# A sparse graph-attention stack on one core: the first layer's weight load placed behind the first edge list

## The chip, the core and the metric

The kernel runs on one core of a Trainium2 chip. The metric is device time in microseconds of one execution, lower is better. Five engines work in parallel, each on its own queue of instructions: TensorE (PE, matmuls), VectorE (DVE), ScalarE (ACT), GpSimd (POOL) and SyncE (SP, which here only issues transfers). DMA engines move data between the device's main memory and the on-chip memories.

## What is computed

The inputs are x (4096 nodes by 512 features), a 4096 by 4096 adjacency of zeros and ones, and weights. Two residual blocks follow each other; cut to what matters:

```python
# layer 0: 8 heads of width 64
h  = einsum('nf,kfp->knp', x, W)
f1 = einsum('knp,kp->kn', h, a[:, :64, 0]); f2 = einsum('knp,kp->kn', h, a[:, 64:, 0])
e  = where(adj > 0, leaky_relu(f2[:, :, None] + f1[:, None, :], 0.2), -1e16)
x  = layernorm(x + heads_side_by_side(softmax(e) @ h))
# layer 1: a graph attention of 8 heads with elu, one of a single head of width 512 with elu,
#          then relu(out @ lin1_w + lin1_b) @ lin2_w + lin2_b
x  = layernorm(x + layer1(x, adj))
```

The adjacency is sparse, with degrees that fall with the index of the node, so tile 0 (the first 128 nodes) has by far the most edges. For each node the sum over its neighbours is all that the softmax needs.

## The kernel before

The kernel works with lists of edges. Nodes come in 32 tiles of 128. It has three stages.

**Stage 1** (`find_edges`, with `beside` for what is done next to it) makes the lists and projects x. The rows of a tile are looked at in *parts*: tile 0 has four (columns 0 to 256, to 1024, to 2304, to 4096), every other tile has one, so there are 35 parts, v = 0 to 34. A part goes through these steps:

- `signs_of` brings the adjacency rows (`raw`) in and ACT turns them into signs (`sg`, L848). For tile 0 this is done in eight pieces ahead of everything else (`sg0`).
- PE makes keys from signs and column numbers (L877, L878) in PSUM.
- DVE searches each segment of columns for its largest keys, eight at a time: MAX8 into `cand` (L884), MATCH_REPLACE8 into `left` (L887), and so on. For tile 0 a segment takes three rounds. `left` has two buffers, and `cand` of tile 0 has one, so that the search of its next part waits for the list of the one before.
- DVE merges the candidates into one sorted list `lst`: MAX8 (L899) and MATCH_REPLACE8 (L901) in turn; part 0 has 13 rounds.
- ACT, POOL and PE turn the list into positions: qs and signs (L906, L909), degs and counts (L911 to L928), a prefix sum prs (L931), sides (L942, L943), s1 (L944), and pl (L960 to L969). ACT copies a column of it, kk (L984). DVE picks the neighbours' numbers (L977 to L988), and POOL writes them to `idx` (L991 to L994).

After the last part of a tile comes `beside(t)`: x's rows of that tile (`xr`) are loaded, transposed on PE (L683), copied by ACT (`xt`, L686), multiplied with the layer's weights on PE (`ph`, L697), copied to a row by ACT (L710) and written to a table in main memory by SP (L711). At t = 8 and t = 16 it loads the weights of the other two attention layers.

`load_projection` brings a layer's weights into `st.w` (eight transfers of 128 KB, L654, for layers of eight heads) and appends columns to them: for each of two attention vectors, broadcast to all partitions (`sab`, L663), and each of four chunks, POOL multiplies weights and vector (`sprod`, L667, 128 by 512 elements) and DVE sums each head's 64 products (L672; L677 for the layer of one head). That makes eight products and eight sums for a layer. `sprod` has two buffers, so a product waits for the sum two before it.

**Order.** In stage 1 the order of each engine's queue is not written by hand. A planner fixes it when the kernel is built: it walks through time by its own estimates of durations, and when an engine is free it takes, of the instructions whose inputs are then ready, the one that stands first in the program. Steps that stand late in the program are taken early where nothing else is ready: the second layer's sums, which stand at tile 8, run from 69 to 78 us here, among the second part of tile 0. On the chip the queue then runs in that order, whatever is late. Memory of closed pools is used again; the buffers of one layer's load lie where those of another did.

**Stages 2 and 3** gather table rows by `idx` with indirect transfers (L1084), weigh them on DVE (L1208) and sum them by matmuls (L1220). Their order is written out in the code, and no line of theirs is touched. The part of stage 1 that the change concerns:

Of the kernel before, what the change touches and what calls it, by code (L numbers as in the profile page):

```python
# [558 lines left out]
def sparse_path(  # L559
# [78 lines left out]
    st0 = Stage2("t0", 8, 64, dest_first=False)  # L638
# [5 lines left out]
    def load_projection(pool, st, w, a):  # L644

        hs, dm = st.heads, st.dim


        st.w = pool.tile([P, FC, 2, st.wide], F32, name=f"sw_{st.name}")
        for c in range(FC):  # L650
            for j in range(2):
                mine = st.w[:, c, j, :HF]
                if hs > 1:
                    nc.sync.dma_start(  # L654
                        mine.rearrange("p (k o) -> p k o", o=dm),
                        w[ts(j, hs // 2), ts(c, P), :].rearrange("k f o -> f k o"),
                    )
                else:
                    nc.sync.dma_start(mine, w[0, ts(c, P), ts(j, HF)])
        with tc.tile_pool(name=f"swload_{st.name}", bufs=2) as wp:  # L660
            for side in range(2):
                ab = wp.tile([P, hs, dm], F32, name="sab")
                nc.sync.dma_start(ab, a[:, ts(side, dm)].partition_broadcast(P))  # L663
                d = (side == 1) == st.dest_first
                for c in range(FC):
                    prod = wp.tile([P, 2, HF], F32, name="sprod")
                    nc.gpsimd.tensor_mul(  # L667
                        prod, st.w[:, c, :, :HF], ab.rearrange("p h d -> p (h d)").rearrange("p (j f) -> p j f", j=2)
                    )
                    if hs > 1:  # L670
                        at = HF if d else HF + hs // 2
                        nc.vector.tensor_reduce(  # L672
                            st.w[:, c, :, at : at + hs // 2],
                            prod.rearrange("p j (h d) -> p j h d", d=dm), AX.X, OP.add,
                        )
                    else:
                        nc.vector.tensor_reduce(st.w[:, c, int(d), HF:], prod, AX.XY, OP.add)  # L677

    def turn_in(sb, ps, st, src, t):

        pt = ps.tile([P, FC, P], F32, name="pt", tag="ph")
        for c in range(FC):
            nc.tensor.transpose(pt[:, c, :], src[:, ts(c, P)], ident)  # L683
        xt = sb.tile([P, FC, P], F32, name="xt")
        for c in range(FC):
            nc.scalar.activation(  # L686
                xt[:, c, :], pt[:, c, :], AF.Copy, accum_out=st.xparts[:, c, t : t + 1]
            )
        return xt

    def project_in(ps, st, columns, n=P):

        halves = []
        for j in range(2):
            ph = ps.tile([P, st.wide], F32, name="ph")
            for c in range(FC):
                nc.tensor.matmul(ph[:n], columns(c), st.w[:, c, j], start=(c == 0), stop=(c == FC - 1))  # L697
            halves.append(ph)
        return halves
# [35 lines left out]
    def project_mean(sb, ps, st):  # L735

        mean = sb.tile([P, FC], F32, name="mean")
        nc.vector.tensor_reduce(mean, st.xparts, AX.X, OP.add)
        nc.vector.tensor_scalar_mul(mean, mean, 1.0 / N)
        project_out(sb, st, project_in(ps, st, lambda c: mean[:, c : c + 1], 1), NT, 1)  # L740
# [99 lines left out]
    def signs_of(sb, t, pieces=1):  # L840

        raw = sb.tile([P, N], I32, name="raw", bufs=2)
        sg = sb.tile([P, N], BF16, name="sg")
        w = N // pieces
        for i in range(pieces):
            nc.sync.dma_start(raw[:, ts(i, w)], adj[ts(t, P), ts(i, w)])
        for i in range(pieces):
            nc.scalar.activation(sg[:, ts(i, w)], raw[:, ts(i, w)], AF.Sign)  # L848
        return sg

    def find_edges(big, sb, ps, pk, constants, sg, beside):
# [12 lines left out]
        for v, p in enumerate(pts):  # L864
            t, k, c0, nch = p.t, p.k, p.first, p.n
# [91 lines left out]
            for lo in range(0, nch, per):  # L957
                m = min(per, nch - lo)
                pl = ps.tile([P, m, k + 2], F32, name="pl")
                nc.tensor.matmul(  # L960
                    pl, ident_b, own_b[:, None, kmax - k :].to_broadcast([P, m, k + 2]), start=True, stop=False
                )
                last = None
                for block, groups, chunks in blocks_in(p, lo, m):
                    for of, w in ((rhs, k + 2), (rest, k + 1)):
                        if last:
                            nc.tensor.matmul(*last, start=False, stop=False)
                        last = pl[:, chunks, :w], s1[:, ts(p.at + block, P)], of[:, groups, :w]
                nc.tensor.matmul(*last, start=False, stop=True)  # L969
                cs = slice(c0 + lo, c0 + lo + m)  # L970
                nc.scalar.copy(nl[:, cs], pl[:, :, k + 1])
                nc.gpsimd.tensor_scalar(hole[:, cs, 0], nl[:, cs], -0.5, FAR, op0=OP.is_lt, op1=OP.mult)
                src = sb.tile([P, longest], F32, name="src")[:, :m]
                sel = sb.tile([P, 512], F32, name="sel")[:, : m * k].rearrange("p (m k) -> p m k", k=k)
                if k < 100:
                    shape = [P, m, k]
                    nc.vector.tensor_tensor(  # L977
                        sel, iota_k[:, lo : lo + m, :k], pl[:, :, k : k + 1].to_broadcast(shape), op=OP.is_equal
                    )
                    nc.vector.tensor_tensor(sel, sel, pl[:, :, :k], op=OP.mult)  # L980
                    nc.vector.tensor_reduce(src, sel, AX.X, OP.add)
                else:
                    kk = sb.tile([P, longest], F32, name="kk")[:, :m]
                    nc.scalar.copy(kk, pl[:, :, k])  # L984
                    for c in range(m):
                        nc.vector.scalar_tensor_tensor(
                            sel[:, c], iota_k[:, lo + c, :k], kk[:, c : c + 1], pl[:, c, :k],
                            op0=OP.is_equal, op1=OP.mult, accum_out=src[:, c : c + 1],  # L988
                        )

                past = sb.tile([P, longest], F32, name="past")[:, :m]  # L991
                nc.gpsimd.tensor_scalar(past, nl[:, cs], -0.5, 2.0 * N, op0=OP.is_lt, op1=OP.mult)
                nc.gpsimd.tensor_add(past, past, src)
                nc.gpsimd.tensor_copy(idx[:, cs], past)  # L994
            if p.last:
                beside(t)

# [21 lines left out]
    def blocks_in(p, lo, m):  # L1019


        out = []
        for i in range(p.blocks):
            mine = [(g, c - lo) for g, c in enumerate((i, p.off + i)) if i < p.chunks[g] and lo <= c < lo + m]
            if len(mine) == 2:
                out.append((i, slice(0, 2), slice(mine[0][1], mine[1][1] + 1, p.off)))
            elif mine:
                g, c = mine[0]
                out.append((i, slice(g, g + 1), slice(c, c + 1)))
        return out  # L1030
# [339 lines left out]
    with ExitStack() as pools:  # L1370
        big = pools.enter_context(tc.tile_pool(name="eb", bufs=1))
        sb = pools.enter_context(tc.tile_pool(name="es", bufs=2))
        sg0 = signs_of(sb, 0, 8)
        constants = edge_constants(big)
        load_projection(big, st0, w0, a0)
        ps = pools.enter_context(tc.tile_pool(name="ep", bufs=1, space=PSUM))
        pp = pools.enter_context(tc.tile_pool(name="eq", bufs=2, space=PSUM))
        pk = pools.enter_context(tc.tile_pool(name="ek", bufs=2, space=PSUM))

        def beside(t):  # L1380
            xr = sb.tile([P, F], F32, name="xr")
            nc.sync.dma_start(xr, x[ts(t, P), :])
            xt = turn_in(sb, pp, st0, xr, t)
            project_out(sb, st0, project_in(pp, st0, lambda c: xt[:, c, :]), t)
            if t % 8 == 7:
                split_s(sb, st0, t - 7, 8)
            if t == 8:
                load_projection(late, st1, w1, a1)
            if t == 16:
                load_projection(late, st2, wo, ao)  # L1390

        find_edges(big, sb, ps, pk, constants, sg0, beside)
        project_mean(sb, pp, st0)
# [224 lines left out]
```

## Time and profile before

| | us |
|---|---|
| median of three runs | 2126.52 (2125.99 to 2130.2) |
| the profiled execution, its own time | 2338.45 |
| its span, first to last instruction | 2336.3 |
| busy: PE / DVE / ACT / POOL | 1771.7 / 1331.3 / 660.7 / 1151.6 |
| mean granted TensorE clock | 0.879 |

The profiled execution is 212 us longer than the median, so its microseconds serve to compare places within it. In a timeline each line gives the start, the duration, the engine, the line of the kernel, the operation, what is written from what, and shapes; in brackets stands how long the engine sat idle before it and what released it. A list of waits gives, for each pair of waiting and releasing lines, the total in microseconds, how often, and the longest.

### The profile page before, as it was taken

What the parts mean: (1) busy time and instruction counts of PE and PEld (TensorE: products, weight loads), DVE (VectorE), ACT (ScalarE), POOL (GpSimd) and SP (SyncE); (2) the same over time, 40 slices, a digit from 0 to 9 for tenths busy, and PEclk for the clock granted to TensorE, in tenths of its full rate; (3) what the DMA queues carried; (4) which work ended last, traced back from release to release, by engine and by line L of the source; (5) the groups of instructions that cost most, each with busy time, mean ns of one, the idle gap of its engine ahead of it and who ended that gap; (6) DMA issues with size and microseconds to landing.
All of it is one profiled execution on the core that took longest, in us unless ns stands there. A gap on an engine that the chain in (4) does not pass through costs nothing.

```text
span 2336.3 us, 29301 instructions
## 1 busy us (share of the span) xinstructions
PE 1771.7 (76%) x8987; PEld 1040.1 (45%) x8987; DVE 1331.3 (57%) x3933; ACT 660.7 (28%) x2316; POOL 1151.6 (49%) x1658
## 2 busy tenths in 40 slices
PE   4777776645677787764667687666999898998997
PEld 3655442213444564432444465434545443444444
DVE  5887777745676797744555676653343424334322
ACT  3446776650222222111222232211111011111221
POOL 5424444456555666536556666536355634445300
PEclk9889997866878899876788899887999998999999
DMA  6434565536666667526555556436254624335301
GB/s 214 132 129 158 219 241 220 213 83 179 181 175 182 197 208 224 166 76 163 154 140 145 159 158 186 133 110 191 85 156 126 172 82 148 101 109 150 90 19 51
DMA packets 132589, 351.94 MB, mean 151 GB/s; under 512 B 41922, under 2 KB 42954, under 8 KB 128454
## 3 DMA queue, kind: packets, MB, share of 16 engines
q0 software_dynamic: 74160, 206.25, 32.5%
q1 hardware_dynamic: 58262, 143.72, 17.3%
q8 instruction: 74, 1.21, 0.2%
q14 instruction: 93, 0.76, 0.1%
HBM read 347.31 MB, written 42.24 MB: 167 GB/s over the span
## 4 chain that ended last, share of the span: by engine, by line
PE 46%; DVE 16%; issue 13%; ACT 7%; another core or an unknown queue 7%; POOL 6%; DMA 4%; SPq 0%; DVEq 0%; POOLq 0%; ACTq 0%
PE acc L1220 15%; PE ph L697 11%; PE p L1495 10%; PE p L1507 5%; DVE g L1208 3%; POOL g L1084 2%; DMA xr<-sx_d 2%; DVE cand L884 2%; DMA g<-table_t,idx 2%; PE pt L683 1%; POOL s L944 1%; DVE cand L901 1%; DVE lst L899 1%; ACT sides L943 1%
## 5 line engine op out<-in xcount | busy, mean ns | idle before, releaser
L1084 POOL DMA_INDIRECT g<-table_t,idx x927 | 937.2, 1011 | 769.4 <-PE acc L1220 336.4
L1220 PE MATMUL acc<-g,sm 128*64 128x260 f32 (+2 forms) x4068 | 587.9, 414 | 175.3 <-DVE g L1208 91.7
L697 PE MATMUL ph<-sw_t,xt 128*128 128x264 f32 (+1 forms) x1536 | 436.4, 437 | 146.5 <-ACT xt L686 80.6
L1220 PEld LDWEIGHTS acc<-g,sm 128*64 128x64 f32 x4068 | 332.9, 146 | 395.1 <-issue 123.9
L697 PEld LDWEIGHTS ph<-sw_t,xt 128*128 128x128 f32 x1536 | 323.0, 217 | 229.2 <-ACT xt L686 97.9
L1208 DVE TENSOR_TENSOR g<-g,wp 128x2048 f32<-128x2048 f32 (+4 forms) x134 | 349.3, 2607 | 37.9 <-ACT wp L1163 18.7
L884 DVE MAX8 cand<-key 128x8 f32<-128x353 f32 (+55 forms) x467 | 196.3, 446 | 79.5 <-PE key L878 78.9
L1495 PE MATMUL p<-sht,sl1w 128*128 128x512 f32 (+1 forms) x576 | 229.0, 553 | 5.5 <-issue 4.9
L1507 PE MATMUL p<-sl2w,shid 128*128 128x512 f32 x512 | 227.2, 598 | 0.0
L686 ACT ACTIVATE xt<-pt 128x128 f32<-128x128 f32 x384 | 101.5, 279 | 292.9 <-PE pt L683 122.1
L710 ACT COPY hrow<-ph 128x260 f32<-128x260 f32 (+2 forms) x194 | 71.9, 374 | 320.2 <-PE ph L697 186.9
L1495 PEld LDWEIGHTS p<-sht,sl1w 128*128 128x128 f32 x576 | 107.7, 191 | 116.9 <-issue 112.0
L1507 PEld LDWEIGHTS p<-sl2w,shid 128*128 128x128 f32 x512 | 95.4, 190 | 120.4 <-issue 119.6
L1257 DVE SCALAR_TENSOR_TENSOR o<-ex,o 128x512 f32<-128x512 f32 x64 | 44.5, 695 | 179.2 <-ACT ex L1256 150.0
L877 PE MATMUL key<-sg,s_identb 128*128 128x512 bf16 (+1 forms) x258 | 111.9, 435 | 14.5 <-DVE cand L884 9.0
L848 ACT ACTIVATE sg<-raw 128x4096 bf16<-128x4096 int32 (+1 forms) x39 | 117.0, 2999 | 9.4 <-PE key L877 5.0
L1498 ACT ACTIVATE shid<-p,sl1b 128x512 f32<-128x512 f32 (+1 forms) x72 | 46.0, 640 | 244.5 <-PE p L1495 221.0
L878 PE MATMUL key<-frac,places 128*128 128x512 bf16 (+1 forms) x258 | 112.0, 435 | 2.6 <-POOL places L784 2.6
L1195 DVE TENSOR_SCALAR sm<-iota_n,nl,w 128x64 f32<-128x64 f32 x339 | 83.5, 328 | 31.9 <-ACT w L1166 31.9
L1155 DVE TENSOR_TENSOR z<-s,g 128x16 f32<-128x16 f32 (+9 forms) x294 | 44.7, 174 | 82.9 <-DMA g<-table_t,idx 81.2
L686 ACT ACTIVATION_READ_ACCUMULATOR xt<-pt 128x1 f32 x384 | 79.9, 208 | 0.0
L1228 DVE RECIPROCAL rd<-acc 128x8 f32<-128x8 f32 x64 | 13.1, 205 | 114.4 <-PE acc L1220 73.3
(184 smaller groups left out, 1812.8 us busy)
## 6 DMA issues: line engine op xcount, KB each, us to landing
raw<-in_adj_dram SPq DMA_DIRECT2D x31, 2048.0 KB
table_t<-hrow SPq DMA_DIRECT2D x64, 260.0 KB
xr<-in_x_dram SPq DMA_DIRECT2D x64, 256.0 KB
g<-table_t,idx POOLq DMA_INDIRECT x927
table_t<-hrow SPq DMA_DIRECT2D x32, 257.0 KB
sx_d<-o SPq DMA_DIRECT2D x32, 256.0 KB
xr<-sx_d SPq DMA_DIRECT2D x32, 256.0 KB
out_dram<-xr SPq DMA_DIRECT2D x32, 256.0 KB
```

Of the source, the lines that this page charges most:

```text
L686: nc.scalar.activation(xt[:, c, :], pt[:, c, :], AF.Copy, accum_out=st.xparts[:, c, t : t + 1])
L697: nc.tensor.matmul(ph[:n], columns(c), st.w[:, c, j], start=(c == 0), stop=(c == FC - 1))
L848: nc.scalar.activation(sg[:, ts(i, w)], raw[:, ts(i, w)], AF.Sign)
L877: nc.tensor.matmul(out_, ident_b, sg[:, j:e], start=True, stop=False)
L878: nc.tensor.matmul(out_, places[:, w], frac[:, j - w * KW : e - w * KW], start=False, stop=True)
L884: nc.vector.max(out=cand[:, at : at + 8], in_=part)
L1084: nc.gpsimd.indirect_dma_start(out=u.g[:, k, : self.st.row], out_offset=None, in_=self.st.table[:, :], in_offset=bass.IndirectOffsetOnAxis ...
L1195: nc.vector.tensor_scalar(sm[:, at + i], of_g, node[k], u.w[:, k], op0=OP.is_equal, op1=OP.mult)
L1208: nc.vector.tensor_mul(body, body, wp[:, :, :, None].to_broadcast(body.shape))
L1220: nc.tensor.matmul(out_[g * HN : (g + 1) * HN], sm[:, slot], rows(k), start=start, stop=stop)
L1495: nc.tensor.matmul(p1, l1w[:, c, ts(k, P)], hts[b][:, c, :n], start=(c == 0), stop=(c == FC - 1))
L1507: nc.tensor.matmul(p2, hids[b][:, k, ts(j, P)], l2w[:, k, :], start=(k == 0), stop=(k == HC - 1))
```

## The change

The call that loads the first layer's weights moves from in front of `find_edges` into it, behind the work on part v = 0, which is the first of tile 0's four lists. Nothing else is edited; in the program all steps of part 0 now stand ahead of the load, and parts 1 to 34 behind it. The PSUM pools are now opened ahead of the load.

```diff
@@ find_edges, at the end of the loop over parts @@
                 nc.gpsimd.tensor_copy(idx[:, cs], past)
+            if v == 0:
+                beside(-1)
             if p.last:
                 beside(t)
@@ the caller @@
         constants = edge_constants(big)
-        load_projection(big, st0, w0, a0)
         ps = pools.enter_context(tc.tile_pool(name="ep", bufs=1, space=PSUM))
         pp = pools.enter_context(tc.tile_pool(name="eq", bufs=2, space=PSUM))
         pk = pools.enter_context(tc.tile_pool(name="ek", bufs=2, space=PSUM))
 
         def beside(t):
+            if t < 0:
+                load_projection(big, st0, w0, a0)
+                return
             xr = sb.tile([P, F], F32, name="xr")
```

## The prediction

> **What bounds the kernel now.** The page comes first: the chain that ended last is spread thin, and 40 slices show three stages. The wait lists and timelines then give the boundaries: edges are listed and x is projected until about 500 us, two attention layers of eight heads run to about 1610, the last layer with its dense part to the end. The change touches only the first stage, so the question is what paces its start. The busy time by stretch answers (columns: start and end, length, then PE, PEld, DVE, ACT and POOL busy with counts, clock, DMA share, GB/s):
>
> ```profile
> 8.00:13.40 5.40, 1.35 (x4) 0.46 (x4) 4.70 (x40) 3.15 (x5) 5.33 (x17) 1.00 1.03 253
> 13.40:31.50 18.10, 6.84 (x17) 4.74 (x17) 7.54 (x26) 1.14 (x8) 13.19 (x71) 1.00 0.83 297
> 31.50:42.10 10.60, 6.96 (x33) 4.98 (x31) 9.74 (x38) 6.22 (x17) 0.00 (x0) 1.00 0.49 163
> ```
>
> VectorE (DVE) is nearly full while it searches part 0, idle for 18.10 - 7.54 = 10.6 us in the middle, then full again. Its list of waits from 10 to 60 us says for what (us, times, longest):
>
> ```profile
> DVE sw_t L672 <- POOL sprod L667: 10.4, 8, 4.6
> ```
>
> All eight are the sums of the first layer's weights. The DVE timeline shows them inside the search of part 0:
>
> ```profile
> 13.30 0.20 DVE L884 MAX8 cand<-left 128x8 f32<-128x43 f32 x1
> 18.12 0.69 DVE L672 TENSOR_REDUCE sw_t<-sprod 128x8 f32<-128x512 f32 x1 [4.61 <-POOL sprod L667]
> 20.35 0.69 DVE L672 TENSOR_REDUCE sw_t<-sprod 128x8 f32<-128x512 f32 x1 [1.55 <-POOL sprod L667]
> ...
> 21.02 0.19 DVE L887 MATCH_REPLACE8 left<-cand,left 128x43 f32<-128x43 f32 x1
> 23.06 0.69 DVE L672 TENSOR_REDUCE sw_t<-sprod 128x8 f32<-128x512 f32 x1 [1.85 <-POOL sprod L667]
> 24.28 0.69 DVE L672 TENSOR_REDUCE sw_t<-sprod 128x8 f32<-128x512 f32 x1 [0.53 <-POOL sprod L667]
> 24.88 0.20 DVE L884 MAX8 cand<-left 128x8 f32<-128x43 f32 x1
> ...
> 41.70 0.36 DVE L899 MAX8 lst<-cand 128x8 f32<-128x192 f32 x1
> ```
>
> Two sums stand ahead of each single step of the search, because the load comes first in the program; the list of part 0 ends at 41.70 + 0.36 = 42.06. What the sums wait for is GpSimd (POOL):
>
> ```profile
> 16.82 1.26 POOL L667 TENSOR_TENSOR sprod<-sw_t,sab 128x512 f32<-128x512 f32 x1 [2.21 <-issue]
> 19.05 1.27 POOL L667 TENSOR_TENSOR sprod<-sw_t,sab 128x512 f32<-128x512 f32 x1
> 21.76 7.38 POOL L667 TENSOR_TENSOR sprod<-sw_t,sab 128x512 f32<-128x512 f32 x6
> ```
>
> From 42 to 190 us DVE is busy 122.06 of 147.90, so a list that ends earlier should pull what follows with it.
>
> **What the Trainium skill says.** "TensorE: Matmul & The Clock Gate", in the section on the array's architecture, says that DVE and ScalarE queues are strict first-in-first-out. The trace agrees: the ready replacement at 21.02 stands behind two late sums. "GPSIMD Engine Reference", section 3.1, gives about 2.6 cycles an element at two inputs, which by its 1.2 GHz is an estimate of 1.1 us for 512 elements; the trace has 1.265 median, and that is used. "VectorE: DVE Perf Modes", in the perf-mode table, has a reduction at its lowest rate only; the trace has 0.686 us for 512 elements, 0.61 from start to start.
>
> **The change part by part.** It removes and adds no instruction. The load's eight weight DMAs, two vector DMAs, eight products (L667) and eight sums (L672) move behind part 0 in the program, which lowers their rank.
>
> SP: part 0 issues no DMA. The ten DMAs follow the eight pieces of the adjacency as before (4.55 to 13.7 us), so nothing changes its place: cost 0 to 0.5 us. If other DMAs slipped ahead, each would cost the 0.4 to 0.5 us of an issue.
>
> POOL: part 0's own work begins at 42.99 with degs, long after the products end at 29.14. One 0.19 us copy (L955) may pass ahead. Products start at 16.82 because the vector's DMA was issued at 12.32; neither moves. Cost 0 to 0.2 us. The two product buffers still tie product n+2 to sum n.
>
> PE and ACT: the first projection (L697, 26.29 to 31.91) needs the last sum, as now; the row copy (L710, 31.94) waits on it, and the list's own ACT step comes behind it. As the sum at 29.17 is paced by POOL, this stays, within the 0.61 us of one sum. The keys of part 2 (L877, 31.70) stand behind that projection on PE; DVE takes them up only at 80.22, so their cover is large.
>
> DVE: this is where the term lies. Where will the sums go at low rank? Into places where the next step of the search depends on the one just issued. The third layer's sums (L677) already have lower rank than part 2 and show it:
>
> ```profile
> 85.03 0.67 DVE L677 TENSOR_REDUCE sw_t<-sprod 128x1 f32<-128x512 f32 x1
> ...
> 85.69 0.26 DVE L887 MATCH_REPLACE8 left<-cand,left 128x116 f32<-128x116 f32 x1
> 86.69 0.69 DVE L677 TENSOR_REDUCE sw_t<-sprod 128x1 f32<-128x512 f32 x1 [0.74 <-POOL sprod L667]
> 87.29 0.27 DVE L884 MAX8 cand<-left 128x8 f32<-128x116 f32 x1
> ```
>
> One sum before and one after the replacement on left: two places a segment, a single sum in each, and DVE still waits there for POOL. At 13.30 the search of part 0 stands at such a place, so I put the first sum where it is now, and its 4.61 us wait stays. What changes is that pairs become singles. From sum 1 to sum 8 there are 29.17 - 18.12 = 11.05 us, of which seven starts take 7 x 0.61 = 4.3 and leave 6.8 for the search. Pairs used it for three steps (about 0.75 us). Singles have seven places, three segments at two and one in the final list: all that the search now does from 29.78 to 31.51 (1.73 us) and the first MAX8 of the list (0.38) fit in, 2.9 us in 6.8. After sum 8, at 29.78, there remain 42.06 - 29.78 - 2.1 = 10.2 us, and the list ends at 40.0. **Gain 2.1 us.**
>
> Bounds on it: zero, if the sums keep their pairs; 10.4, if the whole wait goes. Below zero too, as the stage's order is planned anew. Next to be late is ACT's copy kk (L984), for which DVE waits 17.3 us up to 190. It hangs on part 0's list and moves along. One thing could stop it: the second layer's products start at 67.82 when their vector lands, and DVE reaches the first sum at 69.24. That DMA stands in SP's queue behind row writes that hang on ACT and PE, so I expect it to move along; otherwise the 2.1 us are waited out there.
>
> The sum: profiled execution 2338.45 us (span 2336.3 and 2.15 around it) less 2.1 is 2336.3. That execution stands 212 us above the median of 2126.52; scaled by 0.909 the gain would be 1.9. I take 2.1 whole: 2126.5 - 2.1 = **2124.4**. A measurement here tells about 0.2%, 4.25 us, from no change, so this is no change.
>
> **The rivals.**
> *No effect at all.* The planner puts the sums in the same places, or the gain is waited out at 69 us: 2126.5. For it: the same inputs are ready at the same times.
> *Faster.* The first sum falls behind the search, into the list's rounds (L899 and L901 alternate, 0.42 us a step). Then search and first MAX8 end at about 16.4, seven steps run between the sums, 10.54 - 0.38 - 7 x 0.42 = 7.2 us remain after 29.78, and the list ends at 37.0: 5.1 us, 2121.4. With no wait left, 10.4 us and 2116.1. For it: the second layer's sums (69.24 to 77.73) lie in just such rounds. Against: the third layer's lie in the search.
> *Slower.* A newly planned order puts bursts of projection matmuls ahead of a list's matmuls on PE. The chain has one already: eight ph (3.65 us from 50.67) ahead of pl (L960). A burst of 16 takes 3.83 (36.55 to 40.38). One more gives 3.83 - 2.1 = +1.7, still no change; from two it decides: 7.66 - 2.1 = +5.6, 2132.1; with four, 2139.7. For it: from 190 to 500 us DVE waits 73.2 us for keys from PE, so PE's order sets the pace, and all tiles' order is open. Against: the shift of ranks is small.
>
> **How the numbers follow.** My case with the case of no effect gets 0.42 (2122.5 to 2129), faster 0.27 (2114 to 2122), slower 0.31 (2131 to 2140). The range is 2114 to 2139: it holds all of the likeliest, most of the faster case down to the full wait with 2 us of planning beyond it, and up to four bursts.
>
> **What would show it.** Right: single sums with one or two search steps between them; the wait before the first still above 4 us; last sum near 29.2; list of part 0 ending near 40; stage end (about 500) earlier by 2. Wrong: first L672 behind the first L899, or total wait on L667 below 5 us (faster case); more wait of DVE on L878 or of prs and pl on PE after 100 us (slower case); a stage end moved by over 5 us with part 0 as forecast would make planning, not the move, the cause.

## The result, and the profile after

| | before | after |
|---|---|---|
| median, us (20 runs each) | 2128.08 (2122.86 to 2135.1) | 2132.24 (2127.47 to 2137.28) |
| ratio, 95% interval | 1 | 1.002 (1.0012 to 1.0028) |
| the profiled execution / its span | 2338.45 / 2336.3 | 2131.38 / 2129.6 |

The change makes the kernel slower by 4.2 us: 2124.4 was forecast, and the sign is the other one. The profile of before that the prediction was read from was of an unusually long execution, with a lower granted clock behind stage 1 (0.83 in place of 0.92 from 500 to 1610 us); a second one (below, "before again") took 2124.41 us, and comparisons are made with that.

The same view as before, busy time by stretch (start and end, length, then PE, PEld, DVE, ACT and POOL busy with counts, clock, DMA share, GB/s), of the middle stretch, first of before again, then of the kernel after:

```profile
13.40:31.50 18.10, 7.99 (x27) 5.43 (x27) 8.61 (x30) 2.91 (x11) 13.19 (x71) 1.00 0.75 285
```

```profile
13.40:31.50 18.10, 9.13 (x29) 6.01 (x28) 9.84 (x38) 2.77 (x11) 13.23 (x70) 1.00 0.78 289
```

VectorE does 38 instructions there in place of 30 and is busy 9.84 us in place of 8.61. Its list of waits from 10 to 60 us (total, times, longest; the total is 9.3 in before again) and its timeline say how, in the kernel after:

```profile
DVE sw_t L672 <- POOL sprod L667: 8.0, 8, 3.4
```

```profile
13.29 0.20 DVE L884 MAX8 cand<-left 128x8 f32<-128x43 f32 x1
16.87 0.69 DVE L672 TENSOR_REDUCE sw_t<-sprod 128x8 f32<-128x512 f32 x1 [3.38 <-POOL sprod L667]
...
17.54 0.19 DVE L887 MATCH_REPLACE8 left<-cand,left 128x43 f32<-128x43 f32 x1
19.10 0.69 DVE L672 TENSOR_REDUCE sw_t<-sprod 128x8 f32<-128x512 f32 x1 [1.37 <-POOL sprod L667]
...
27.80 0.69 DVE L672 TENSOR_REDUCE sw_t<-sprod 128x8 f32<-128x512 f32 x1 [0.45 <-POOL sprod L667]
...
28.47 0.35 DVE L899 MAX8 lst<-cand 128x8 f32<-128x192 f32 x1
```

One sum stands at a place where two stood, the search of part 0 goes on between them, and the merge of the list starts right behind the eighth sum. Its last MAX8 starts at 38.67, in before at 41.70 (40.56 in before again). The beginning is thus as forecast, and yet the whole is longer.

To see where the time goes, take one mark of each part: the start of its first count on GpSimd (degs, L911), read from that engine's timeline (us from the span's start). For part 34, in before again and then in after:

```profile
488.99 0.19 POOL L911 TENSOR_SCALAR degs<-balance 128x1 f32<-128x1 f32 x1 [0.88 <-ACT signs L909]
```

```profile
493.24 0.19 POOL L911 TENSOR_SCALAR degs<-balance 128x1 f32<-128x1 f32 x1 [0.88 <-ACT signs L909]
```

| part | before again | after | after less before again |
|---|---|---|---|
| 0 | 41.85 | 39.97 | -1.88 |
| 2 | 120.94 | 118.25 | -2.69 |
| 3 | 162.25 | 160.72 | -1.53 |
| 4 | 172.06 | 173.19 | +1.13 |
| 8 | 234.06 | 235.82 | +1.76 |
| 16 | 318.18 | 322.26 | +4.08 |
| 34 | 488.99 | 493.24 | +4.25 |

A gain of some 2 us is made in part 0, held to part 2, and lost between parts 2 and 16; from there the distance stays between 3.6 and 5.1 us.

Both columns are of single executions. A second profile of the kernel after ("after again") has part 2 at 121.16 and part 34 at 495.91, 0.22 and 6.92 us behind before again. The loss behind part 2 is thus in both profiles of after; the gain ahead of it, and with it the sum at the end, differs between them. What follows stage 1 shows no steady part in it: from the first gather (L1084; L1086 in the kernel after) to the end of the span it takes 1622.8 us in before again, 1626.1 in after and 1622.8 in after again.

### The profile page after: what moved, and what is told of

The parts are those of the page before. It is cut to its first block, busy times and chain, and to the rows that moved or that the text cites. A ratio compares the mean times of both kernels' runs of the same rounds, so it can differ in the third digit from the quotient of the medians.

```text
span 2129.6 us, 29314 instructions
## 1 busy us (share of the span) xinstructions
PE 1723.8 (81%) x8987; PEld 1003.3 (47%) x8987; DVE 1326.5 (62%) x3933; ACT 664.0 (31%) x2316; POOL 1151.8 (54%) x1658
## 4 chain that ended last, share of the span: by engine, by line
PE 37%; DVE 20%; issue 13%; POOL 12%; DMA 11%; ACT 5%; SPq 0%; POOLq 0%; DVEq 0%; ACTq 0%
PE acc L1222 11%; PE p L1500 10%; DMA g<-table_t,idx 9%; PE ph L697 7%; POOL g L1086 7%; DVE g L1210 5%; PE p L1512 4%; DVE cand L884 2%; DMA xr<-sx_d 2%; POOL s L944 1%; DVE sm L1189 1%; DVE cand L901 1%; DVE bs L1263 1%; ACT sides L943 1%; PE key L878 1%
## 5 line engine op out<-in xcount | busy, mean ns | idle before, releaser
L1086 POOL DMA_INDIRECT g<-table_t,idx x927 | 937.8, 1012 | 560.5 <-issue 232.6
L697 PE MATMUL ph<-sw_t,xt 128*128 128x264 f32 (+1 forms) x1536 | 397.8, 407 | 45.2 <-ACT xt L686 45.1
L697 PEld LDWEIGHTS ph<-sw_t,xt 128*128 128x128 f32 x1536 | 294.0, 198 | 114.8 <-ACT xt L686 66.9
L884 DVE MAX8 cand<-key 128x8 f32<-128x24 f32 (+54 forms) x467 | 196.4, 445 | 82.4 <-PE key L878 82.0
L710 ACT COPY hrow<-ph 128x260 f32<-128x260 f32 (+2 forms) x194 | 70.8, 372 | 155.4 <-PE ph L697 154.9
L1165 ACT ACTIVATE wp<-z 128x32 f32<-128x32 f32 (+4 forms) x134 | 27.4, 205 | 202.4 <-DVE g L1210 202.0
L1517 DVE TENSOR_TENSOR xr<-p,xr 128x512 f32<-128x512 f32 x32 | 22.0, 688 | 94.3 <-PE p L1512 93.9
```

Of the source, the lines that this page charges most:

```text
L884: nc.vector.max(out=cand[:, at : at + 8], in_=part)
L1086: nc.gpsimd.indirect_dma_start(out=u.g[:, k, : self.st.row], out_offset=None, in_=self.st.table[:, :], in_offset=bass.IndirectOffsetOnAxis ...
```

## The experiments

The two programs issue the same instructions, and in stages 2 and 3 in the same order. In stage 1 the planner's result differs far beyond the eight sums: against the kernel "singles" below, 243 of PE's 1427 steps stand elsewhere in the kernel after, 163 of VectorE's 1157, 127 of ScalarE's 678, 26 of GpSimd's 728 and 16 of SyncE's 134. So the move has two effects to be told apart: the sums singly in place of pairs, and a newly planned order of everything else. The experiments fix queues by hand. `pin` adds no wait; it tells the planner only that each named instruction comes behind the one named before it on the same engine:

```diff
         project_mean(sb, pp, st0)
+        pin(tc, QUEUES)    # stage 1 only; an engine that isn't named is planned as usual
```

### The kernel before, once more

> The kernel before, profiled again, since its first profile ran 212 us longer than its median. Theory A (the loss lies in stage 1): with the clock as in the changed kernel's profile, the last of the 35 counts (L911) starts about 4 us earlier than the 493.2 of the changed kernel, and the stretch from the first gather to the end is as long as there (1626 us) within 3 us. Theory B (the loss lies behind stage 1): the last count starts within 1 us of 493.2, and the stretch behind it is about 3 us shorter than there.

2124.41 us, span 2122.3. The first product starts at 15.67 (16.82 in the first profile), the eight sums wait 9.3 us (10.4). The last count comes 4.25 us earlier than in after, as theory A has it. The stretch from the first gather to the end is 3.3 us shorter, as theory B has it, but after again has the same 1622.8 us there, so that difference is one between executions.

### The sums alone, and the order alone

"singles" is the kernel before with all five queues held to their own order, but the eight sums one at a place, as the kernel after has them (the number is the width of the segment):

```diff
-DVE: sum 1, sum 2, L887 (43), sum 3, sum 4, L884 (43), sum 5, sum 6, L887 (48), sum 7, sum 8, L884 (48), L884 (23),
-     L887 (48), L884 (48), L887 (23), L884 (23), L887 (23), L884 (23), L899
+DVE: sum 1, L887 (43), sum 2, L884 (43), L887 (48), L884 (48), L884 (23), sum 3, L887 (48), sum 4, L884 (48), L887 (23),
+     sum 5, L884 (23), sum 6, L887 (23), sum 7, L884 (23), sum 8, L899
```

"pairs" is the converse: the kernel after with all its queues held to its own order, but the sums in pairs, two at each of the first four places.

> The kernel before with every queue of stage 1 held to its own planned order, except that the eight sums of the first layer's weights stand on DVE where the changed kernel has them (one at a place instead of two). Theory A (the new places gain, the newly planned order of all else loses more): 3 to 5 us faster than before, ratio 0.9975 to 0.9987; the list of part 0 ends near 39, as in the changed kernel, and the lead is kept to the end of stage 1. Theory C (a later wait absorbs any lead of part 0): the list ends near 39, the lead is gone by part 5, ratio 1.000. Theory D (the new places themselves cost): 4 us slower, ratio 1.002.

> The changed kernel with every queue of stage 1 held to its own planned order, except that the eight sums stand on DVE in pairs, as before the change. Theory A: 3 us slower than the changed kernel, 7 us slower than before, ratio 1.003 to 1.0035. Theory C: as the changed kernel, ratio 1.002. Theory D: as the kernel before, ratio 1.000.

> The changed kernel, timed on the same chip beside the others. All theories: about 4 us slower than before, ratio 1.001 to 1.003. Its trace gives a second reading of where its lead of 3 us at part 0 goes: theory A has it lost between parts 2 and 4 again, where PE runs the projection's matmuls (L697) ahead of a list's (L967).

Ratios to before: singles 0.9995 (0.9987 to 1.0002), after again 1.0024 (1.0016 to 1.0032), pairs 1.0046 (1.0034 to 1.0059). The sums alone don't cost anything; the order alone costs more than the change as a whole. Singles was expected to be 3 to 5 us faster than before: the list and the kept lead came as in its theory A, but whole executions show no such gain. Pairs is the slowest, as in theory A, and by more than it had (1.003 to 1.0035). The marks of singles show what becomes of the early gain: against before again they are 1.65 us earlier at part 0, 2.48 at part 2 and 2.40 to 2.52 at every part from 3 to 34. Nothing absorbs it.

In these profiles the place of the sums is worth more in the new order than in the old: the count of part 0 comes at 45.42 in pairs, against 39.97 in after. PE's timelines of pairs, after and singles, in this order:

```profile
28.92 0.59 PE L877 MATMUL key<-sg,s_identb 128*128 128x512 bf16 x1 [10.04 <-DVE left L887]
...
30.58 4.88 PE L697 MATMUL ph<-sw_t,xt 128*128 128x264 f32 x16
```

```profile
24.00 0.59 PE L877 MATMUL key<-sg,s_identb 128*128 128x512 bf16 x1 [4.16 <-DVE left L887]
...
25.66 5.51 PE L697 MATMUL ph<-sw_t,xt 128*128 128x264 f32 x16
```

```profile
25.15 5.10 PE L697 MATMUL ph<-sw_t,xt 128*128 128x264 f32 x12 [6.16 <-issue]
30.09 0.38 PE L877 MATMUL key<-sg,s_identb 128*128 128x512 bf16 x1
```

In the new order the keys of part 2 stand ahead of the first projection, in the old one behind most of it. They wait until the search of part 0 has read the last of its keys (L887 into `left`), and with the sums in pairs the search is late: the projection, whose last sum ends at 27.96, starts at 30.58. The Trainium skill, "TensorE: Matmul & The Clock Gate", section "The mechanism" of its part on packing, has matmuls in strict first-in-first-out order; this agrees. In pairs ScalarE's row copy (L710) then waits for that projection, and the list of part 0 ends at 40.16 (39.03 in after), but its qs (L906) starts behind the copies, at 44.59 (39.13 in after). By these timelines the pairs themselves cost the list 1.1 us, and the place of the keys ahead of the projection costs another 4.3.

### One engine's queue of the order before

The kernel after with PE's queue alone, or VectorE's alone (with single sums), held to the order of the kernel before; the others are planned around it.

> The changed kernel, with PE's queue in stage 1 alone held to the order of the kernel before; the other four queues are planned anew around it (28 of 678 ACT steps and 174 of 1157 DVE steps stand elsewhere than before the change). Theory E (PE's new order makes the loss: list matmuls and keys behind projection matmuls): the loss is gone, last count (L911) at 487 to 490, ratio 0.999 to 1.000. Theory F (the loss lies in DVE's new order, which puts searches of the next part where the neighbours' pick waits for kk): last count stays near 493, ratio 1.002.

> The changed kernel, with DVE's queue in stage 1 alone held to that of the kernel before with the sums one at a place (the DVE order of the run called singles); the other queues are planned anew, and come out nearly as before the change (12 of 1427 PE steps and 4 of 678 ACT steps stand elsewhere). Theories E and F both: as singles within 1 us, last count near 486.5 to 487.5, ratio 0.999 to 1.000. If it is near 493 instead, the loss sits in those few steps or in the place of the call itself.

PE's order: ratio 0.9985 (0.9974 to 0.9996), so in whole executions the loss is gone, which speaks against theory F. Its one profile, of an execution 4.6 us above this kernel's median, has the last count at 491.05, later than theory E allows (see "Open"). VectorE's: 1.001 (0.9999 to 1.0022), which can't be told from before and is little under after. Its last count is 492.52, where both theories had 486.5 to 487.5. Neither run isolates its engine, as the planner follows with the others: with VectorE held, only 12 steps of PE still stand elsewhere than in singles. From part 2 on that kernel takes the time of the old order (table below). What it loses, it loses ahead of part 2, by another step, on GpSimd (timelines of after with VectorE's order, then of singles):

```profile
67.14 9.88 POOL L667 TENSOR_TENSOR sprod<-sw_t,sab 128x512 f32<-128x512 f32 x8 [9.22 <-DMA sab<-in_a_dram]
81.51 1.26 POOL L667 TENSOR_TENSOR sprod<-sw_t,sab 128x512 f32<-128x512 f32 x1 [4.50 <-DMA sab<-in_ao_dram]
82.85 0.19 POOL L911 TENSOR_SCALAR degs<-balance 128x1 f32<-128x1 f32 x1
```

```profile
63.27 9.96 POOL L667 TENSOR_TENSOR sprod<-sw_t,sab 128x512 f32<-128x512 f32 x8 [7.07 <-DMA sab<-in_a_dram]
76.60 0.19 POOL L911 TENSOR_SCALAR degs<-balance 128x1 f32<-128x1 f32 x1 [3.37 <-ACT signs L909]
77.99 1.26 POOL L667 TENSOR_TENSOR sprod<-sw_t,sab 128x512 f32<-128x512 f32 x1 [0.80 <-DMA sab<-in_ao_dram]
```

The second layer's vector lands later (its products start at 67.14 in place of 63.27), and a product of the third layer that waits 4.50 us for its own vector has been planned ahead of part 1's count: that count comes at 82.85 in place of 76.60. Part of these 6.25 us is older: at part 0 this execution is already 1.63 us behind singles, its first product having started 1.17 later. When part 1's signs end on ScalarE it is 3.78 behind (80.30 against 76.52), and the product ahead of the count does the rest.

### Without the wait for GpSimd

"products first" is singles with two more changes, made together: the eight products stand in a row on GpSimd, ahead of the constants that lay between them, and SyncE loads the first of the two vectors behind the second of the eight weight pieces instead of behind the eighth. "products shared" also gives VectorE the products of the odd chunks.

```diff
-POOL: ..., constants, product 1, constants, product 2, constants, products 3 to 8, ...
+POOL: ..., products 1 to 8, constants, ...
-SP: weight pieces 1 to 8, vector 1, vector 2, ...
+SP: weight pieces 1 and 2, vector 1, weight pieces 3 to 8, vector 2, ...
```
```diff
-                    nc.gpsimd.tensor_mul(
+                    (nc.vector if st is st0 and c % 2 else nc.gpsimd).tensor_mul(
```

> Singles, with two queues edited by hand: on POOL the eight products run ahead of the constants that stood between them, and on SP the two vectors are loaded behind the first and the last piece of the weights instead of both last. All else is as in singles. Theory A (POOL's products pace the list of part 0, and whatever part 0 wins is kept to the end): products start near 14.9 and end near 25, the list of part 0 ends at 36 to 37, 2 to 3 us ahead of singles, the last count at 484, 4.5 to 5.5 us faster than before, ratio 0.9975. Theory C (later waits absorb more than 2.4 us of lead): last count 486.5 as in singles.

> As products_first, with the four products of odd chunks moved from POOL to DVE, which waits at that place anyway. Theory A: DVE has 9.8 us of search steps, products and sums from 13.5 on and about 1 us of wait, the list of part 0 ends near 34 to 35.5, last count at 482 to 483, 6 to 7.5 us faster than before, ratio 0.9965 to 0.997. Rival: with PE's order unchanged its projections stand ahead of part 0's prs (L931), which can't start before about 38, so that the lead of part 0's list over products_first is absorbed and the last count stays at 484.

Ratios to before: products first 0.9962 (0.9949 to 0.9975), median 2122.66 against 2129.33, and products shared 0.9971 (0.9961 to 0.9981). Both beat the kernel before and the kernel after. Timelines of products first, GpSimd and then VectorE:

```profile
14.67 9.84 POOL L667 TENSOR_TENSOR sprod<-sw_t,sab 128x512 f32<-128x512 f32 x8
```

```profile
24.55 0.69 DVE L672 TENSOR_REDUCE sw_t<-sprod 128x8 f32<-128x512 f32 x1 [0.45 <-POOL sprod L667]
...
35.42 0.36 DVE L899 MAX8 lst<-cand 128x8 f32<-128x192 f32 x1
```

The eighth sum comes 3.49 us earlier than in singles (28.04), the list's end 3.48, and the count of part 34 3.27 (483.28 against 486.55). What is saved at part 0 with the order held fast arrives at the end of the stage, so theory C is out. Taking four products off GpSimd brings no more: the list ends at the same place (last MAX8 at 35.49), since VectorE now has products and sums to do in turn. From 13.5 to 25.3 us it waits only once, for 0.43 us, and its four products take 4.55 us. The last count at 484.28 is the figure of the rival, but not for its reason: the list has no lead over products first that could be absorbed.

### Which half of the new order costs the time

Each program has one planned sequence over all engines. "old then new" follows singles' up to the count of part 2 and takes what is left in the order of the kernel after; "new then old" is the converse.

```diff
-QUEUES = singles' order, whole             # or after's, whole
+QUEUES = X's order up to part 2's count, then what is left in Y's order
```

> The changed program with its stage-1 queues held to singles' order up to the count of part 2 (118.46 us there) and to the changed kernel's own planned order from there on; no work is left out. Theory O (the loss lies in the order in which parts 3 to 15 are planned): the count of part 0 at about 40.2, of part 2 at 118.5, then part 4 near 173, part 15 near 312 and part 34 near 493, ratio to before 1.002. Rival L (the loss is made by the order up to part 2, which leaves transfers and row copies behind for later): part 34 near 486.5, ratio 0.9995. If both halves matter only together, part 34 lies near 490 and the ratio near 1.000 to 1.001.

> The converse: the changed kernel's own planned order up to the count of part 2, singles' order from there on; no work is left out. Theory O: the count of part 2 near 118.3, part 4 near 169.6, part 15 near 305.6, part 34 near 486.5, ratio to before 0.9995 (0.9985 to 1.0005). Rival L: part 4 near 173, part 34 near 493, ratio 1.002. If both halves matter only together, part 34 lies near 490.

These two, and "one step" below, were run on another chip, where the kernel before took 2333.74 us; in the profile of old then new the granted clock is 0.84 from 500 to 1610 us, against 0.92 in before again. So only their ratios and the marks of stage 1 are used. Old then new 1.003 (1.0013 to 1.0047), new then old 0.9999 (0.9986 to 1.0012): as theory O has it, the order behind part 2 carries the loss, and the order ahead of it none that these runs show. The two are the changed program and differ in nothing but the order of queues, so the place of the call and of the pools is not what costs. The marks fall into two groups, with PE's order held between them:

| stage-1 order behind part 2 | kernel | part 2 | part 34 | part 2 to 34 |
|---|---|---|---|---|
| of before | before again | 120.94 | 488.99 | 368.05 |
| | singles | 118.46 | 486.55 | 368.09 |
| | products first | 115.28 | 483.28 | 368.00 |
| | products shared | 116.41 | 484.28 | 367.87 |
| | new then old | 120.81 | 489.61 | 368.80 |
| nearly that of before | after, VectorE's order held | 124.46 | 492.52 | 368.06 |
| PE's held, others planned | after, PE's order held | 119.12 | 491.05 | 371.93 |
| of after | after | 118.25 | 493.24 | 374.99 |
| | after again | 121.16 | 495.91 | 374.75 |
| | old then new | 119.41 | 494.52 | 375.11 |
| | pairs | 125.00 | 500.41 | 375.41 |

The start differs between kernels by up to 10 us, and between executions of the same queues by up to 3; the stretch from part 2 to part 34 takes 367.9 to 368.8 us with the order of before and 374.7 to 375.4 with that of after, whatever went before. **The new order costs 6.9 us there.** The TensorE clock is not the cause: from 120 to 500 us it is 0.86 to 0.88 in all these profiles, and 0.87 in products first and pairs alike. What the order is paid in shows in VectorE's list of waits from 118 to 500 us, singles first, then after:

```profile
DVE cand L884 <- PE key L878: 71.2, 58, 3.8
DVE sel L986 <- ACT kk L984: 7.7, 5, 3.5
DVE sel L977 <- ACT nl L971: 5.2, 5, 1.9
DVE sel L986 <- PE key L878: 2.9, 1, 2.9
```

```profile
DVE cand L884 <- PE key L878: 76.3, 58, 4.5
DVE sel L986 <- ACT kk L984: 12.9, 7, 3.7
DVE sel L977 <- ACT nl L971: 6.4, 6, 2.0
```

Keys come late by 5.1 us more. kk and nl cost 6.4 us more, against which the 2.9 us of the fourth line are gone. In these lines together that is 8.6 us more of waiting. The list of before again is that of singles to within 0.2 us a line, and after again has 75.7, 12.9 and 5.7. Both lists cover the same 382 us although after is not as far on at the end, so the sum needn't equal 6.9.

### One place of the new order, mended

The largest jump is between parts 3 and 4: 9.80 us in singles, 12.47 in after. Most of it is given back at once: from part 4 to 5 singles takes 18.40 us and after 16.23. Counted from part 2, after is 1.6 us behind singles at part 5, 4.4 at part 8 and 6.7 at part 16. VectorE's timelines at the jump, of singles and of after:

```profile
165.16 0.46 DVE L899 MAX8 lst<-cand 128x8 f32<-128x312 f32 x1
...
169.10 0.33 DVE L986 SCALAR_TENSOR_TENSOR sel<-iota_k,kk,pl 128x112 f32<-128x112 f32 x1 [3.48 <-ACT kk L984]
```

```profile
169.67 0.33 DVE L986 SCALAR_TENSOR_TENSOR sel<-iota_k,kk,pl 128x112 f32<-128x112 f32 x1 [3.67 <-ACT kk L984]
...
170.68 0.48 DVE L899 MAX8 lst<-cand 128x8 f32<-128x312 f32 x1
```

The last MAX8 of part 4's list stands ahead of the picks of part 3 in one order and behind them in the other, so that in the new one it sits out their wait for kk. "One step" is the kernel after with its own order and this MAX8 alone moved ahead of the four picks; "two steps" also moves that list's qs and signs on ScalarE (L906, L909) ahead of the row copy (L710).

```diff
-DVE: ..., L901, L986 x4, L899, L884, ...
+DVE: ..., L901, L899, L986 x4, L884, ...
-ACT: ..., kk L984, L710, L717, qs L906, signs L909, ...        (two steps only)
+ACT: ..., kk L984, qs L906, signs L909, L710, L717, ...
```

> The changed kernel with its stage-1 queues held to their own planned order, but for one step: the last MAX8 of part 4's list (L899) goes on DVE ahead of the four picks of the part before (L986), which wait 3.67 us for ACT's copy kk; no work is left out. Theory G (that step is what costs part 4 its 3.5 us): the list ends near 166.0 in place of 171.16, the count of part 4 comes near 170.3 in place of 173.19, and part 34 earlier by up to 2.9, near 490.5; ratio 1.0005 to 1.001. Rival H (ACT's queue has a row copy, L710, in front of that list's qs, and the copy waits for eight projection matmuls on PE to 172): the list ends near 166.0 but the count stays at 172.9 to 173.2, part 34 near 493, ratio 1.002.

> The kernel of the run before (the last MAX8 of part 4's list ahead of the four picks on DVE) with one more step moved: ACT takes that list's qs and signs (L906, L909) ahead of the row copy L710 that waits for PE; no work is left out. If those two steps are what part 4 lost, qs starts at 169.3 in place of 172.29 and the count of part 4 comes near 170.2 in place of 173.06. Theory O1 (the loss of part 4 passes on whole): part 34 near 490 in place of 492.89, ratio to before 1.001. Rival O2 (PE's planned order takes it back: the prefix sum prs of part 4 stands behind further projection matmuls, so part 5 comes no earlier): part 5 near 189.2, part 34 near 493, ratio 1.002 to 1.0025.

One step: 1.0026 (1.0012 to 1.004), nothing won. ScalarE's timeline of it:

```profile
171.97 0.38 ACT L710 COPY hrow<-ph 128x260 f32<-128x260 f32 x1 [2.53 <-PE ph L697]
...
172.29 0.35 ACT L906 ACTIVATE qs<-lst,value 128x56 f32<-128x56 f32 x1
```

The list is now done at 166.3 in place of 171.2, but qs stands behind a row copy that waits for eight projection matmuls, and the count comes at 173.06. This is rival H. Two steps: 1.0018 (1.0006 to 1.003), count at 173.17. In this execution part 3 was 0.85 us later than in after, so parts 3 to 4 take 11.60 us in place of 12.47. qs starts right behind kk, as expected, but kk itself comes at 171.13 (169.27 in one step). Of these 1.86 us, 1.08 is the later part 3. The rest lies on PE, where the matmuls just ahead took longer this time (two of the projection 1.20 us in place of 0.67, one of pl 0.30 in place of 0.21). And the count waits for a third queue, as GpSimd's timeline of two steps shows:

```profile
172.90 0.19 POOL L994 CAST idx<-past 128x4 int32<-128x4 f32 x1
173.17 0.19 POOL L911 TENSOR_SCALAR degs<-balance 128x1 f32<-128x1 f32 x1
```

The signs end at 171.86, but the new order has part 3's idx, which hangs on the late picks, ahead of this count; in singles the count stands first (169.65, idx at 171.57). Even so something is won: from part 2 to part 5 two steps takes 69.41 us, as singles does (69.59; after 71.17). It is lost again by part 6 (90.52; singles 86.80, after 89.93). Part 2 to part 34 takes 374.75 us in one step and 375.44 in two steps, as in after; this, and not the ratio, speaks against theory O1. At this place the new order has no single late step: what was mended uncovered the next queue's, and what was won by part 5 was gone by part 6.

## Why the prediction was right about part 0 and wrong about the sum

**The places of the sums: right.** The first stays where it was, behind the MAX8 at 13.29, and then one stands at each place: two in the first segment, two in the second, three in the third and one ahead of the list. Sums 1 to 8 take 27.80 - 16.87 = 10.93 us (11.05 forecast), GpSimd paces them, and all the search fits between them as counted. Only the first MAX8 of the list does not: it was to stand ahead of sum 8 and stands behind it (28.47).

**The wait before the first sum above 4 us: 3.38.** It is 3.47 in before again and 4.27 in after again, and follows the start of the first product (15.58, 15.67 and 16.48). The mechanism is as told, the size is that of one profile.

**The gain of 2.1 us at the list: right but for the first MAX8.** The list ends at 40.92 in before again, at 39.26 in singles, whose first product starts within 0.02 us of it: 1.66 us. The forecast was 1.73 for the search and 0.38 for the MAX8 that did not move ahead. After gives 39.03, of which 0.09 is an earlier product. The second layer's products moved along, as forecast (63.27 in singles, 65.70 in before again), so the lead was not waited out there; by the end of the stage it is 2.44. In whole executions it can't be told from zero: 0.9995 of before is -1.1 us, with an interval from -2.8 to +0.4.

**SyncE and GpSimd at no cost: held.** The products start at 15.58 and 17.81 and then run six in a row for 7.38 us, as before; the copy L955 did pass ahead (14.65), at no cost.

**PE, "the keys of part 2 stand behind that projection": failed.** They moved ahead of it (24.00 against 25.66). With single sums that cost nothing here; with pairs it costs 4.3 us at part 0.

**"A list that ends earlier should pull what follows with it": the step that failed.** As a statement on the queues as they stood it is right, to 0.12 us over 32 parts (singles). But the sum applied it to queues that the same edit had redrawn. The term for the new order was set at nothing, with "the shift of ranks is small" against it; it measured 374.99 - 368.05 = +6.9 us. Less the 2.4 us that singles wins in the old order, that makes +4.5; the medians give +4.2, and the ratio of after again, 1.0024, gives +5.1.

**The slower rival: right in where the cost comes from, its mechanism not found.** It put the price on PE's planned order, and VectorE does wait more for keys, by 5.1 us, one of the signs it named. But at the one place looked at no burst of that size is newly put ahead of a list: the eight projection matmuls at part 4 run in both orders (3.84 us from 168.54 in singles, 3.69 from 169.15 in after), and the late steps there lie on VectorE, ScalarE and GpSimd. Whether the other places are alike is not shown. Its figure for two bursts, 2132.1, falls on the measured 2132.24 by luck: it is 5.6 us above 2126.5, and two such bursts were not found. The test named in the prediction, a stage end moved by over 5 us with part 0 as forecast, is met against singles, which holds the order of before (+6.7), though not against before again itself (+4.25).

**The faster rival: not what happened, but within reach.** The sums stayed in the search, yet the wait that it priced is there to be had. Products first takes 3.5 us of it by hand, on top of the single sums.

**Open.** Which displacements cost how much behind part 4 was not taken apart, and so neither was PE's share against that of the other engines. With PE's order held, the median is 0.15% below before, while its profile takes 371.93 us from part 2 to 34 and has part 34 at 491.05, 2.06 us behind before again; the two don't agree, and no run settles it.

## What to carry to other kernels

Where a planner fixes the order, moving a block in the program is two changes: the block's own place, and a new order of all that is planned behind it. Price the second by holding the queues fast: the old order with only the wished-for move, and the new order without it, tell the two apart in one comparison. When the first pays and the second costs, as here, keep the old order and make the move by hand; in singles and products first, where the order was held, the early gain arrived at the end undiminished.

## What the runs showed that was not expected

The time between two marks some 370 us apart followed the order of the queues closely: with the order of before it was 368.0 us to within 0.13 in four kernels whose starts differ by 5.7 us, and 368.8 in new then old; with that of after it was 375.1 to within 0.35 in four profiles whose starts differ by 6.8. The first 120 us are less steady: executions of the same queues differ by 2.9 us at part 2 (118.25 and 121.16). And on VectorE a product of 512 elements took 0.67, 1.02, 1.61 and 1.25 us in the one kernel that has them there; what stretched the later ones was not tried.
